# Attention on one core: a unit's row maxima computed beside the exponentials of the unit before it, without a lead of three score fills

## The chip, the cores and the metric

The kernel runs on one core of a Trainium2 chip. The metric is the device time of one execution in microseconds (us). Before the change three runs took 1225.27, 1232.97 and 1233.84 us, median 1232.97 us.

## The reference

Input `x` is 8 batches of 1024 tokens of width 256, float32. The reference is a block of three parts:

```
x = x + 0.5 * ffn(layernorm(x))      # 8 experts, top 2, each expert kept only if at most 1280 tokens chose it
x = x + attention(layernorm(x))      # 16 heads of width 16, causal
x = x + 0.5 * ffn(layernorm(x))
```

An expert that more tokens chose than its capacity is left out altogether. The kernel counts the choices while it computes the attention, and runs the expert part only if some expert is kept; in the profiled execution none is, so that all the time goes to the attention with its layer norms, gates and projections:

```
q, k, v = x @ Wq.T + bq, x @ Wk.T + bk, x @ Wv.T + bv
attn    = softmax(causal(q * 0.25 @ k.T))
out     = (attn @ v) @ Wo.T + bo
```

## The kernel before, in words

**Units.** The attention is cut into NU = 32 units: unit u is batch b = u // 4 and group g = u % 4 of four heads. Each unit has two kinds of score fills, 18 of each, and a fill is one step of the schedule:

- A maxima fill (`m_steps`, L831) multiplies queries by keys into a pair of PSUM banks, tile `sm`, and VectorE reduces it to row maxima, tile `mx` (L870). Fills 0 to 17 belong to two halves of the queries, hf = 0 and hf = 1; the last one of half 0 is fill 6, that of half 1 is fill 17.
- An exponential fill (`e_steps`, L928) computes the scores again, transposed, tile `sc`, and adds the negated maxima to them in TensorE (L947: `take_m` times the rows 62 to 66 of `neg`). ScalarE takes the exponential into `pT` (L966), GpSimd masks blocks on the diagonal, and `values` (L1000) multiplies `pT` by the values into `pav`. Fills E0 to E4 are half 0, E5 to E17 are half 1. E5 is the first that reads the maxima of half 1.

`sm` and `sc` share one PSUM pool of three pairs (L605): a fill can start when the reader of the fill three places earlier is done.

**From maxima to rows.** When a half's maxima are complete, `settle` (L888) runs four small VectorE operations (`mxr`, two on `mneg`, the transpose to `mside`) and starts `send` (L911). `send` issues two DMAs of 16 KB from ScalarE's queue: `rows` (SBUF to DRAM) and, when that has landed, `neg` (DRAM into the four rows of `neg`). `start(steps, lag)` (L1229) sets the step at which a sequence goes on: (3 * lag + 2) // 4 steps later. So `rows` is issued 2 steps after `mside`, and `neg` 5 steps after `rows`. Both stand in ScalarE's instruction order: while ScalarE's queue waits to issue `neg`, no later exponential is issued.

**Order of the work.** Everything is put into one hand-made order per engine (`Lane`, L615). Unit u's loop (L1311) runs "EMEMEM" six times: an exponential fill of unit u, then a maxima fill of the stream, 36 steps. The stream (`maxima`, L1245) goes through the maxima fills of all units in turn. Before unit 0 it runs the 18 fills of unit 0 alone; beside unit 0's exponentials it runs those of unit 1. At the start of unit 1 three more maxima fills are run alone (L1307 to L1309), so that from there on the stream is three fills ahead: beside unit u's exponentials stand fills 3 to 17 of unit u + 1 and fills 0 to 2 of unit u + 2. In unit 30 the stream ends three fills early, and unit 31 has exponentials only. Every third step `gap` (L1205) adds pieces of other work: the projections `pq` (L740), the values `pv`, the output projection `px`, the transposes `pta` of the normed input (`enter`, L716), and the products `pav` that have come due. `take(side)` adds small VectorE work, `settle` first.

**Loads.** SyncE's queue issues all large DMAs in order: `parts` (a projection's result to DRAM, four of 256 KB for each chunk, `project`), `qk` (back into SBUF, four of 512 KB for each unit: two tensors for each of two head pairs, `fetch`, L769), `sums`, `on`, `few`, `rs` (division by the row sums), `x_a` and `out_dram`. Unit u + 2's `qk` go to one of three buffers, whose last reader is unit u - 1; they are started 6 steps into unit u, and 5 steps apart.

Of the kernel before, what the change touches and what calls it, by code (L numbers as in the profile page):

```python
# [29 lines left out]
def macaron_kernel(  # L30
# [568 lines left out]
    def attention(run_no, src, dst, gate0, logits, tally):  # L599
        NU = B * NG  # L600
# [3 lines left out]
        with stack:  # L604
# [29 lines left out]
            def pair(name):  # L634
                return ps_pair.tile([P, 2, 512], F32, tag="pair", name=name)
# [10 lines left out]
            def matmul(out, lhsT, rhs, start=True, stop=True):  # L646
                on.tensor.matmul(out, lhsT=lhsT, rhs=rhs, start=start, stop=stop)
# [183 lines left out]
            def m_steps(u):  # L831
                q, k = qks[u % 3][:, 0], qks[u % 3][:, 1]

                def fill(hf, pieces):
                    sm = pair("sm{}_{}_{}_{}".format(u, *pieces[0][:3]))
                    ends = [at + (ib + 1) * P - j0 for ib, j0, pr, at in pieces if (ib + 1) * P - j0 <= 512]
                    for n, (ib, j0, pr, at) in enumerate(pieces):
                        w = min(512, (ib + 1) * P - j0)
                        for h in range(2):
                            r = 64 * h  # L840
                            matmul(
                                sm[:, h, at : at + w],
                                q[r : r + 64, pr, ib * P : (ib + 1) * P],
                                k[r : r + 64, pr, j0 : j0 + w],
                                start=(n == 0),
                                stop=not ends,
                            )
                    for c in range(2 if ends else 0):
                        for h in range(2):
                            r = 64 * h  # L850
                            at = ends[0] - P + 64 * c
                            part, mask = sm[:, h, at : at + 64], masked[r : r + 64, :]
                            if len(ends) == 2:
                                blocks = sm[:, h].rearrange("p (n w) -> p n w", w=P)[:, :, 64 * c : 64 * c + 64]
                                i0, i1 = (e // P - 1 for e in ends)
                                part = blocks[:, i0 : i1 + 1 : i1 - i0]
                                mask = mask.unsqueeze(1).to_broadcast([64, 2, 64])
                            matmul(part, before_k[r : r + 64, c, :], mask, start=False, stop=(c == 1))
                    mx = mx_tiles[u % 3][hf]
                    ib, j0, pr, at = pieces[0]  # L860
                    own = j0 == 512 * hf
                    if len(pieces) == 1:
                        g = (0, 2, 1, 3)[ib % 4]
                        out, in_ = mx[:, :, pr, g, (0 if own else (0, 1, 3, 1)[ib % 4])], sm
                    elif pieces[1][2] == pr:
                        flat = mx[:, :, pr].rearrange("p h g s -> p h (g s)")
                        out, in_ = flat[:, :, 3:7], sm.rearrange("p h (n w) -> p h n w", w=P)
                    else:
                        out, in_ = mx[:, :, :, 2, 0], sm.rearrange("p h (n w) -> p h n w", w=2 * P)
                    on.vector.tensor_reduce(out, in_, AX.X, ALU.max)  # L870

                plain = [(1, [(ib, 0, pr, 0)]) for ib in range(4, 8) for pr in range(2)]
                masked_ones = []
                for hf in range(2):
                    i, j0 = 4 * hf, 512 * hf
                    masked_ones.append([(hf, [(i + 3, j0, pr, 0)]) for pr in range(2)])
                    masked_ones[hf] += [(hf, [(i, j0, pr, 0), (i + 2, j0, pr, P)]) for pr in range(2)]
                    masked_ones[hf] += [(hf, [(i + 1, j0, 0, 0), (i + 1, j0, 1, 2 * P)])]
                if u == 0:
                    todo = masked_ones[0] + plain + masked_ones[1]  # L880
                else:
                    rest = deque(masked_ones[0] + masked_ones[1])
                    plain = deque(plain)
                    todo = [(plain if n % 3 == 1 or not rest else rest).popleft() for n in range(18)]
                steps = [lambda a=a: fill(*a) for a in todo]
                done = max(n for n, a in enumerate(todo) if a[0] == 0)

                def settle(hf):  # L888
                    mx = ap.tile([P, 4, 2, 2], F32, tag="mxr", name=f"mxr{u}_{hf}")
                    on.vector.tensor_reduce(  # L890
                        mx.rearrange("p x b a -> p x a b"),
                        mx_tiles[u % 3][hf].rearrange("p h r (a b) s -> p (h r) a b s", a=2),
                        AX.X,
                        ALU.max,
                    )
                    yield
                    mx = mx.rearrange("p (h r) b a -> p h (r b a)", h=2)
                    neg = ap.tile([P, 2, 2, 8], F32R, tag="mneg", name=f"mneg{u}_{hf}")
                    high, low = neg[:, :, 0], neg[:, :, 1]
                    on.vector.tensor_scalar(high, mx, -1.0, None, ALU.mult)  # L900
                    yield
                    on.vector.scalar_tensor_tensor(
                        low.bitcast(F32), mx, -1.0, high.bitcast(F32), ALU.mult, ALU.subtract
                    )
                    yield
                    turned = ap.tile([P, 32], F32, tag="mside", name=f"mside{u}_{hf}")
                    on.vector.transpose(turned, neg.bitcast(F32).rearrange("p x c i -> p (x c i)"))
                    start(send(hf, turned), 3)
                    yield

                def send(hf, turned):  # L911
                    rows = passing.tile([8, 512], F32, tag="rows", name=f"rows{u}_{hf}")
                    on.scalar.dma_start(out=rows.rearrange("c (i s q) -> s c i q", i=4, s=4), in_=turned)
                    yield 6
                    on.scalar.dma_start(
                        out=negs[u % 2][hf][62:66, :, :512].bitcast(F32),
                        in_=rows.rearrange("(p r) s -> p r s", r=2),
                    )

                return steps, settle, done  # L920


# [295 lines left out]
            def step(fill, every, rate, small):  # L1218
                due()
                fill()  # L1220
                count[0] += 1
                small, urgent[0] = max(small, urgent[0]), 0
                for _ in range(small):
                    if take(side):
                        break
                if count[0] % every == 0:
                    gap(rate)

            def start(steps, lag=0):  # L1229
                timed.append([count[0] + (3 * lag + 2) // 4, steps])  # L1230

            def due():
                for entry in list(timed):
                    while entry[0] <= count[0]:
                        lag = next(entry[1], None)
                        if lag is None:
                            timed.remove(entry)
                            break
                        entry[0] = count[0] + (3 * lag + 2) // 4
# [20 lines left out]
            for u in range(-1, NU):  # L1260
                b, g = divmod(u, NG)
                rate, every = 17 / 12, FILLS
                if u < 0:
                    rate, every = 23 / 9, 2
                elif g == 0:
                    spare[0] = False
                    if b == 0:
                        work.append(project(0, 1))
                        rate = 8 / 3
# [18 lines left out]
                elif g == 3:  # L1288
# [5 lines left out]
                    if b + 1 == B:  # L1294
# [3 lines left out]
                        rate = 8 / 3  # L1298
# [4 lines left out]
                if u < 0:  # L1303
                    for _ in range(18):
                        step(maxima, every, rate, 1)
                else:
                    if u == 1:  # L1307
                        for n in range(3):
                            step(maxima, every, rate, n)  # L1309
                    es = deque(e_steps(u))  # L1310
                    for k, which in enumerate("EMEMEM" * 6):  # L1311
                        small = 3 if k % 6 in (1, 5) else 0
                        if which == "E":
                            step(es.popleft(), 2 if u + 1 == NU else every, rate, 0 if u + 1 < NU else 2)
                        elif stream[0] < 18 * NU:
                            step(maxima, every, rate, small)
# [81 lines left out]
```

## Time and profile before

| | before |
|---|---|
| three runs, us | 1225.27, 1232.97, 1233.84 (median 1232.97) |
| the profiled execution, us | 1243.32 |
| span of its trace, us | 1241.2 |
| mean granted TensorE clock | 0.964 |
| busy, us (share of the span): TensorE | 1143.7 (92%) |
| VectorE | 939.9 (76%) |
| ScalarE | 739.6 (60%) |
| GpSimd | 434.8 (35%) |
| maxima reductions on VectorE (`mx`) | 576, mean 1216 ns |
| exponentials on ScalarE (`pT`) | 576, mean 1023 ns |

How to read it: PE is TensorE's matmuls, PEld its weight loads, DVE VectorE, ACT ScalarE, POOL GpSimd, SP SyncE; a q behind a name is the engine's queue, which issues DMAs. In a timeline, a row is a run of equal instructions: start and length in us, engine, line, operation, result <- operands, shapes, number, and in brackets how long the engine had been idle before it and what ended that. A wait put down to "issue" is one for which the profile shows no releaser. All operations that go through `Lane` carry line L623. PEclk is the clock that TensorE was granted, as a share of its full clock. Times are from the start of the span.

### The profile page before, as it was taken

What the parts mean: (1) busy time and instruction counts of PE and PEld (TensorE: products, weight loads), DVE (VectorE), ACT (ScalarE), POOL (GpSimd) and SP (SyncE); (2) the same over time, 40 slices, a digit from 0 to 9 for tenths busy, and PEclk for the clock granted to TensorE, in tenths of its full rate; (3) what the DMA queues carried; (4) which work ended last, traced back from release to release, by engine and by line L of the source; (5) the groups of instructions that cost most, each with busy time, mean ns of one, the idle gap of its engine ahead of it and who ended that gap; (6) DMA issues with size and microseconds to landing.
All of it is one profiled execution on the core that took longest, in us unless ns stands there. A gap on an engine that the chain in (4) does not pass through costs nothing.

```text
span 1241.2 us, 36200 instructions
## 1 busy us (share of the span) xinstructions
PE 1143.7 (92%) x15178; PEld 668.6 (54%) x15178; DVE 939.9 (76%) x1649; ACT 739.6 (60%) x955; POOL 434.8 (35%) x773
## 2 busy tenths in 40 slices
PE   4698999999999998999899998999989999999982
PEld 2455555555565554655456555655546555555541
DVE  2487668878698777888688787988778886798923
ACT  3155676666576565675566655765656655665650
POOL 2434233343344233442334433342344413232331
PEclk9698999999899998999999999999999999999997
DMA  3634674363555545353653635555553545543201
GB/s 108 234 123 167 208 224 130 119 231 105 189 153 158 187 153 189 119 182 134 214 168 112 221 112 194 148 161 189 164 192 113 185 137 182 156 126 105 83 19 38
DMA packets 108501, 190.25 MB, mean 153 GB/s; under 512 B 24736, under 2 KB 42280, under 8 KB 108328
## 3 DMA queue, kind: packets, MB, share of 16 engines
q1 hardware_dynamic: 96776, 184.54, 45.6%
q10 hardware_dynamic: 11552, 3.29, 1.2%
q8 instruction: 122, 2.00, 0.6%
q14 instruction: 51, 0.42, 0.1%
HBM read 94.50 MB, written 93.31 MB: 151 GB/s over the span
## 4 chain that ended last, share of the span: by engine, by line
PE 79%; DVE 10%; DMA 4%; issue 3%; ACT 2%; POOL 1%; ACTq 0%; SPq 0%; POOLq 0%; DVEq 0%
PE sc L623 23%; PE pav L623 21%; PE sm L623 16%; PE pq L623 8%; DVE mx L623 7%; PE px L623 4%; PE pv L623 4%; DMA rows<-mside 3%; PE pta L623 2%; ACT pT L623 1%; DMA parts<-low 1%; DVE mneg L623 0%; DVE st_a L623 0%; DVE xn_a L623 0%; DMA qk<-parts 0%
## 5 line engine op out<-in xcount | busy, mean ns | idle before, releaser
L623 DVE TENSOR_REDUCE mx<-sm 128x2 f32<-128x1024 f32 (+2 forms) x576 | 685.2, 1216 | 211.9 <-PE sm L623 186.0
L623 ACT ACTIVATE pT<-sc 128x1024 f32<-128x1024 f32 x576 | 575.0, 1023 | 329.7 <-PE sc L623 284.6
L623 POOL TENSOR_SCALAR_AFFINE_SELECT pT<-pT 128x256 f32<-128x256 f32 (+1 forms) x448 | 190.7, 440 | 496.0 <-ACT pT L623 485.4
L623 PE MATMUL pav<-pT,vaug 128*32 128x256 f32 (+3 forms) x4608 | 325.8, 390 | 1.4 <-ACT att L623 1.4
L623 PE MATMUL sm<-qk 64*128 64x512 f32 (+3 forms) x1536 | 266.9, 385 | 38.3 <-issue 20.7
L623 PE MATMUL sc<-neg,take_m 64*128 64x512 f32 x1152 | 266.8, 459 | 6.9 <-DVE mx L623 3.5
L623 PE MATMUL sc<-qk 64*128 64x512 f32 (+3 forms) x1536 | 230.9, 337 | 0.0
L623 PEld LDWEIGHTS sm<-qk 64*128 64x128 f32 x1536 | 142.1, 189 | 139.1 <-issue 69.8
L623 PEld LDWEIGHTS pav<-pT,vaug 128*32 128x32 f32 x4608 | 113.6, 109 | 103.4 <-issue 54.7
L623 PEld LDWEIGHTS sc<-neg,take_m 64*128 64x128 f32 x1152 | 110.5, 188 | 100.4 <-issue 50.3
L623 PEld LDWEIGHTS sc<-qk 64*128 64x128 f32 x1536 | 147.6, 188 | 16.5
L623 POOL TENSOR_TENSOR low<-whole,high 128x512 f32<-128x512 f32 x64 | 82.0, 1281 | 157.1 <-ACT high L623 146.2
L623 PE MATMUL sm<-masked,before_k 64*128 64x128 bf16 (+1 forms) x1280 | 87.2, 215 | 0.0
L623 PE MATMUL pq<-xnT,wkT 128*32 128x256 f32 x1024 | 75.7, 405 | 0.0
L623 PE MATMUL px<-woT,on 128*32 128x264 f32 x1024 | 73.7, 387 | 0.9 <-ACT on L623 0.9
L623 PE MATMUL pv<-wvT,xnT 128*32 128x264 f32 x1024 | 74.0, 391 | 0.0
L623 PE MATMUL pq<-xnT,wqT 128*32 128x256 f32 x1024 | 72.7, 389 | 0.5 <-ACT xnT L623 0.5
L623 PEld LDWEIGHTS <-before_k 64*128 64x128 bf16 x1280 | 38.3, 97 | 43.8 <-issue 27.5
L623 POOL TENSOR_TENSOR x_a<-x_a,bo_all 128x512 f32<-128x512 f32 x32 | 41.5, 1301 | 57.5 <-DVE xn_a L623 36.5
L623 PE MATMUL pta<-ident,xn_a 128*32 128x128 f32 (+1 forms) x912 | 33.9, 278 | 18.3 <-DVE xn_a L623 18.1
L623 PEld LDWEIGHTS pq<-xnT,wkT 128*32 128x32 f32 x1024 | 34.4, 115 | 28.0 <-issue 10.8
L623 PEld LDWEIGHTS pq<-xnT,wqT 128*32 128x32 f32 x1024 | 33.2, 112 | 27.8 <-issue 10.8
(128 smaller groups left out, 734.3 us busy)
## 6 DMA issues: line engine op xcount, KB each, us to landing
qk<-parts SPq DMA_DIRECT2D x124, 512.0 KB
parts<-high SPq DMA_DIRECT2D x128, 256.0 KB
parts<-low SPq DMA_DIRECT2D x128, 256.0 KB
sums<-att SPq DMA_DIRECT2D x62, 256.0 KB
x_a<-in_L_attn_x_dram SPq DMA_DIRECT2D x16, 512.0 KB
out_dram<-x_a SPq DMA_DIRECT2D x16, 512.0 KB
on<-sums SPq DMA_DIRECT2D x30, 256.0 KB
rs<-inv SPq DMA_DIRECT2D x30, 256.0 KB
```

The costliest lines, as they stand in the source:

```text
L623: i = call(*args, **kwargs)
```

## The change

Three edits:

1. The three maxima fills at the start of unit 1 are taken out. The stream is then exactly one unit ahead: beside unit u's exponentials stand fills 0 to 17 of unit u + 1. The fills themselves stay the same in number and form.
2. For the last unit, `rows` is started with lag 1, not 3: 1 step after `mside`, not 2.
3. For the last unit, `neg` follows `rows` with lag 4, not 6: 3 steps later, not 5.

```diff
                     on.vector.transpose(turned, neg.bitcast(F32).rearrange("p x c i -> p (x c i)"))
-                    start(send(hf, turned), 3)
+                    start(send(hf, turned), 3 if u + 1 < NU else 1)
                     yield
...
                     on.scalar.dma_start(out=rows.rearrange("c (i s q) -> s c i q", i=4, s=4), in_=turned)
-                    yield 6
+                    yield 6 if u + 1 < NU else 4
                     on.scalar.dma_start(
                         out=negs[u % 2][hf][62:66, :, :512].bitcast(F32),
...
                 else:
-                    if u == 1:
-                        for n in range(3):
-                            step(maxima, every, rate, n)
                     es = deque(e_steps(u))
```

In the order of instructions of the changed program, ScalarE's `rows` of half 1 stands behind E0 of the unit that needs it (before: behind E15 of the unit ahead), and `neg` behind E3 (before: behind E0). For half 0 `rows` stands behind E7 and `neg` behind E10 of the unit ahead (before: E4 and E7). Some pieces of the work that `gap` and `take(side)` place move by a few steps as well: in units with g = 1 the projection's last chunk stands behind E2 instead of E4, in units with g = 2 the first chunk behind E5 instead of E7, both halves of `out_dram` come ahead of `sums` on SyncE, and in units with g = 0 the normed inputs `xn_a` for the last `pta` stand on VectorE directly behind one `mx`, with no `settle` ahead of them.

## The prediction

> **What bounds the kernel now.** I read the page first (engine shares, the slices, the chain that ended last), then the waits of TensorE (PE), then the timelines around the longest of them.
>
> ```profile
> PE   4698999999999998999899998999989999999982
> PEclk9698999999899998999999999999999999999997
> ...
> PE 79%; DVE 10%; DMA 4%; issue 3%; ACT 2%; POOL 1%; ACTq 0%; SPq 0%; POOLq 0%; DVEq 0%
> ```
>
> From slice 4 to the last but one PE is busy nine tenths of the time, and it carries 79% of the chain. So the end moves only by what PE idles, and by what it loses when its clock falls. The waits of PE (releaser: us in total, times, longest):
>
> ```profile
> PE sm L623 <- issue: 20.7, 7, 4.1
> PE pta L623 <- DVE xn_a L623: 18.1, 9, 6.7
> ...
> PE sm L623 <- ACT pT L623: 4.5, 4, 2.1
> ...
> PE sc L623 <- DMA neg<-rows: 1.7, 1, 1.7
> ```
>
> The first line is one place in six units: the third maxima fill of the lead (fill 2 of unit u + 2, the first on the second head pair) stands at the end of the units with g = 2, ahead of its fourth `qk` load. PE's timeline there, and the windows behind all six (us; busy PE, PEld, DVE, ACT, POOL; PEclk; DMA share; GB/s):
>
> ```profile
> 762.17 0.50 PE L623 MATMUL sm<-qk 64*128 64x512 f32 x2 [3.47 <-issue]
> ```
> ```profile
> 326.30:332.60 6.30, 6.29 (x50) 3.37 (x54) 3.08 (x5) 1.53 (x2) 0.41 (x1) 0.50 0.48 179
> 472.80:479.40 6.60, 6.60 (x54) 3.56 (x58) 3.37 (x7) 1.86 (x2) 0.41 (x1) 0.51 0.39 146
> 618.00:622.70 4.70, 4.70 (x36) 2.66 (x38) 1.55 (x3) 0.77 (x1) 0.00 (x0) 0.50 0.52 199
> 762.10:766.10 4.00, 3.93 (x32) 2.15 (x34) 1.55 (x3) 0.30 (x1) 0.00 (x0) 0.57 0.53 202
> 906.10:909.50 3.40, 3.37 (x26) 1.68 (x28) 1.55 (x3) 0.00 (x0) 0.00 (x0) 0.51 0.55 206
> 1049.60:1056.20 6.60, 6.60 (x54) 3.55 (x58) 3.35 (x7) 1.88 (x2) 0.41 (x1) 0.50 0.34 129
> ```
>
> After each gap the granted clock stands near one half for 3.4 to 6.6 us: a gap costs its length and about 2.5 us more.
>
> **What the change gives (us of PE's time).**
> - A. The six gaps at the lead's third fill: 2.99, 4.07, 3.86, 3.47, 3.73, 2.17, together 20.3. After the change that fill comes six steps later, about 6 us at some 36 us for 36 steps, more than the longest gap: the load has landed. Gain 20.3.
> - B. The half clock behind them: length times the missing share, 3.15 + 3.23 + 2.35 + 1.72 + 1.67 + 3.30 = 15.4.
> - C. Six waits of `pta` for `xn_a`, 1.31 each (at 668.74, for one), are 7.9 of the 18.1. VectorE runs `settle` of half 0 ahead of that `xn_a` (0.22 + 0.18 + 0.62 + 0.21, about 1.25); in the changed order no settle stands there. Gain 7.9.
> - D. ScalarE waits at the issue of `neg` for `rows` to land, and the exponential behind it holds a PSUM pair (`sm <- ACT pT`, 4.5, with 1.7 of half clock after 138.0). I take 5; it may also stay, since `rows` keeps its lag: bounds 0 and 6.2.
> - E. The last unit's 1.73 wait for `neg`, 1.7 of half clock behind it. With the shorter lags its `rows` stands one step and its `neg` three steps sooner than the new place alone would give, which makes up for half of the six steps that the maxima come later, while units ahead of it make up for none. I take 1, bounds -3 (a stall of 3 in place of the 1.73, both with clock behind) and 3.4 (both gone).
>
> Sum of the gains 20.3 + 15.4 + 7.9 + 5 + 1 = 49.6. The three fills taken from the start of unit 1 run in unit 30, where PE has other work beside them just as there: 0.
>
> **What it takes.** E5 of every unit needs `neg` of half 1, which is now issued behind E3 of the same unit. Before, it was issued behind E0, with some 10 us to spare. What is left is read from unit 18: the scores of E3 end at 732.57, E5 begins at 735.63.
>
> ```profile
> 732.17 0.40 PE L623 MATMUL sc<-qk 64*128 64x384 f32 x4
> ...
> 735.63 0.40 PE L623 MATMUL sc<-neg,take_m 64*128 64x512 f32 x2
> ```
>
> That is 3.06; in other units 2.6 to 3.1 (2.2 to 2.4 in units 28 and 30). Behind E5 stand PE's maxima fills and products, so all of PE waits, and DVE and ScalarE after it. The transfer is quick when nothing is ahead of it, and slow otherwise. From the chain of waits (start, length):
>
> ```profile
> 397.27 7.13 DMA rows<-mside
> ...
> 976.09 7.00 DMA rows<-mside
> ...
> 1183.07 2.11 DMA neg<-rows
> ```
>
> Both transfers are 16 KB. What makes 7 of 2: SyncE's queue shortly before one `neg`, and that `neg` on ScalarE's queue:
>
> ```profile
> 267.18 1.22 SPq L623 DMA_DIRECT2D parts<-high  x2
> 268.54 1.97 SPq L623 DMA_DIRECT2D parts<-low  x2
> 270.57 1.50 SPq L623 DMA_DIRECT2D qk<-parts  x1
> ```
> ```profile
> 271.08 0.63 ACTq L623 DMA_DIRECT2D neg<-rows  x1
> ```
>
> In the DMA view of 271.1 to 275.6 only SyncE's queue shows packets:
>
> ```profile
> q1 hardware_dynamic: 475, 1.07, 80.7%
> ```
>
> ScalarE's queue (q10) shows its twelve packets from 275.6 to 276.6. So `neg` landed some 5.4 after its issue, when what SyncE had issued ahead of it was through. Four `parts` of 256 KB hold it about 1.4 each.
>
> - F. Units 7, 11, ..., 27 (g = 3; 6). Four `parts` are issued 4.5 to 6.4 after the unit's start (769.53 and 770.90 where it starts at 764.5); the new `neg` follows at about 7.0. The `parts` are through at about 11.3, it lands at 12.0 to 12.7, and E5 wants it at 9.4: stall 2.6 to 3.3, I take 2.9. Gaps of 2.12 (at 135.51) and 2.17 (at 1047.39) were followed by half clock, gaps of 0.9 to 1.3 were not; so 2.4 more. 5.3 x 6 = 32 (bounds 8, with 1.3 a unit, to 41).
> - G. Units 1 and 2, whose chunks stand behind E1, in the same way: 4.5 x 2 = 9 (4 to 14).
> - H. Units 6, 10, ..., 26 (g = 2; 6). Both halves of `out_dram` (512 KB each), `sums` and `qk` are issued ahead of `neg`: by the same rate a stall of about 2.2, and half clock after some of them, 0.8 on average: 3.0 x 6 = 18 (0 to 30).
> - I. The 17 other units: quiet transfer 2.11 against 2.2 to 3.1. I take 0.25 each, 4 (0, if always quiet, to 48 with a loaded one, see below).
>
> ScalarE's wait at `neg` delays what stands behind it, the exponential E4, only as long as `rows` is late; that is in D. POOL's masks follow the exponentials and wait for nothing new. The moved pieces of projections and `values` are the same instructions on the same engines; their cover is PE's own work, 0.
>
> Losses 32 + 9 + 18 + 4 = 63; net 63 - 49.6 = +13.5. The profiled execution would go from 1243.3 (span 1241.2 and 2.1 around it) to about 1257. It was 10 longer than the median of the runs; against 1232.97 the sum gives 1246.5, and I say 1247.
>
> [...] The gaps of 2.12 and 2.17 above lost half the clock. [...] The empty stretch of q10 from 271.1 to 275.6 shows a small transfer kept behind large ones. [...]
>
> **The rivals.**
> - Quick `neg` (ends faster). If `neg` lands within the 2.6 to 3.1 after E3 in nearly all units, F, G and H are gone and I is 4 to 10: 1233 - 49.6 + 7 = 1190. For it: the 2.11 at 1183.07. Against it: 7.13, 7.00 and the stretch from 271.1. It is decided by one number, the time from the issue of `neg` to its landing in units with g = 3: under 3 it is this case.
> - Cancelled out. `out_dram` is issued late enough, or its 512 KB packets let `neg` pass: H is 0, and 63 - 18 - 49.6 = -4.5, about 1229. For it: the order of SyncE's and ScalarE's queues in time is not fixed by the program. Against it: `sums` and `qk` are large as well.
> - Loaded everywhere. If `qk` loads of SyncE's queue, which fill the DMA for much of each unit (45.6% on the page), hold `neg` to about 4.5 in the other 17 units too, each has a stall of 1.6 to 1.9 and 1.0 of clock: 17 x 2.8 - 4 = 44 more, 1290. For it: 5.55 at 1096.48, in the last batch. Against it: `qk` of a unit are 5 steps apart, and in the mean engines are idle half the time.
> - That the change does not do what it says can be left out: the order of the instructions shows the fills moved.
>
> **How the numbers follow.** What a measurement of this kernel can tell from no change is about 1%, 12.3 us. The forecast has 0.42 (own range 1238 to 1262; of this 0.32 slower by over 1%, 0.10 within), cancelled out 0.22 (within 1%), quick `neg` 0.20 (faster), loaded everywhere 0.16 (slower). So faster 0.20, within 0.32, slower 0.48. The range from 1189 to 1285 leaves out about half of the quick and half of the loaded case, 0.18 in all.
>
> **What would show it.** A and B: no `sm` wait put down to "issue" in the g = 2 units, and no half clock at their ends. C: PE's waits for `xn_a` fall by six. F to H: a new line "PE sc <- DMA neg<-rows" among PE's waits, some 14 times 2 to 3 us, at E5, with half clock behind it. If that line is under 15 us in all, the losses are wrong; if the first line stays near 20, the gains are.

## The result, and the profile after

The changed kernel takes 1305.78 us, median of six runs (1297.09 to 1310.24), against 1233.4 (six runs, 1225.27 to 1237.16): ratio 1.0588, 95% interval 1.054 to 1.0637. It is slower, as forecast, but by 72 us and not by 13. The profiled execution took 1297.09 (span 1295.2), so the two traces differ by 54.0. The trace of before is one of its longer executions and that of after the shortest of six. The executions of both kernels spread, and the shorter ones have the higher granted clock: those of the kernel before, also in later runs, had spans from 1226.9 (clock 0.972) to 1242.1 (0.961), those of the changed one from 1295.2 (0.950) to 1308.4 (0.946). What follows accounts for the 54; the other 18 lie in executions that left no trace.

The page of after, busy slices of PE, its clock, and the chain that ended last:

```profile
PE   4798989989999899998999899998999899999983
PEclk9598989989999898999999899998989989999997
...
PE 68%; DMA 14%; DVE 13%; issue 2%; POOL 1%; ACT 1%; SPq 0%; ACTq 0%; POOLq 0%; DVEq 0%
```

PE's share of the chain fell from 79% to 68%, DMA's rose from 4% to 14%, and the dips of the clock come more often. PE's waits of after (releaser: us in total, times, longest):

```profile
PE sc L623 <- DMA neg<-rows: 61.8, 23, 5.5
...
PE pta L623 <- DVE xn_a L623: 10.5, 3, 6.7
...
PE sc L623 <- DVE mx L623: 9.1, 14, 2.3
...
PE sm L623 <- ACT pT L623: 0.7, 1, 0.7
```

The line `sm <- issue` (20.7 before) is gone, `pta` fell by 7.6 and `sm <- ACT pT` by 3.8: the gains came as forecast. In their place stands the wait for `neg`, 1.7 before and 61.8 now. By the page, PE's idle time rose by 32.9 (97.5 to 130.4) and its busy time by 21.1 (1143.7 to 1164.8), with the same number of instructions. Of these 21.1, 14.5 is clock: half of the time that PE was busy in half-clock pieces is 29.2 before and 43.7 after. The other 6.6 is not. Matmuls of `sc <- neg` at full clock add 191.7 after and 184.1 before, most of the difference at E5 (240 ns each in place of 133), where the first of them follows a wait.

Where the 61.8 lie is read from the timelines. In unit 5 (g = 1, starts at 263.33) SyncE's queue, ScalarE's queue and PE show:

```profile
263.07 0.57 SPq L623 DMA_DIRECT2D parts<-high  x1
264.44 0.57 SPq L623 DMA_DIRECT2D parts<-low  x1
265.36 0.57 SPq L623 DMA_DIRECT2D parts<-high  x1
265.98 1.11 SPq L623 DMA_DIRECT2D parts<-low  x1
...
271.57 1.21 SPq L623 DMA_DIRECT2D parts<-high  x2
272.94 1.95 SPq L623 DMA_DIRECT2D parts<-low  x2
```
```profile
266.55 0.54 ACTq L623 DMA_DIRECT2D rows<-mside  x1
...
273.59 0.65 ACTq L623 DMA_DIRECT2D neg<-rows  x1
```
```profile
278.64 0.79 PE L623 MATMUL sc<-neg,take_m 64*128 64x512 f32 x2 [5.04 <-DMA neg<-rows]
```

`rows` is issued behind four `parts` (the first rows) and lands 7.0 us later; only then can ScalarE issue `neg`, now behind four more `parts`, and E5 starts 5.05 after that. PE has waited 5.04. Two windows of this trace (us; busy PE, PEld, DVE, ACT, POOL; PEclk; DMA share; GB/s): while `neg` is under way the DMA engines are half busy, and behind the wait the clock is at one half:

```profile
273.00:277.00 4.00, 0.59 (x6) 0.19 (x2) 1.23 (x1) 1.02 (x1) 1.26 (x3) 0.87 0.50 148
```
```profile
278.70:282.80 4.10, 4.10 (x36) 2.35 (x36) 1.23 (x1) 1.02 (x1) 0.25 (x1) 0.50 0.69 262
```

The same for all units, from PE's timeline at E5 and the half-clock pieces there. These are 3.41 or 6.83 us long, and the long ones begin while PE still waits, so that only the time in which PE was busy counts (half of it is lost). The wait of unit 19 (2.33) ended with a reduction `mx`, not with `neg`. The last column is what the prediction had for these units, under the letters of its terms:

| units | waits at E5, us | sum | clock lost | together | forecast |
|---|---|---|---|---|---|
| g = 1: 5, 9, ..., 25 | 5.04 4.86 3.70 5.14 5.45 5.43 | 29.6 | 12.9 | 42.5 | 1.5 (in I) |
| g = 3: 7, 11, ..., 27 | 2.88 3.00 2.13 2.33 2.63 2.10 | 15.1 | 7.7 | 22.8 | 32 (F) |
| g = 2: 6, 10, ..., 26 | 2.23 2.30 1.25 0.96 0 0.95 | 7.7 | 3.4 | 11.1 | 18 (H) |
| 1 and 2 | 3.96 2.89 | 6.9 | 4.6 | 11.5 | 9 (G) |
| eleven others | up to 1.59 | 3.6 | 0 | 3.6 | 2.8 (in I) |
| 31, the last | 1.48 | 1.5 | 1.7 | 3.2 | in E |

### The profile page after: what moved, and what is told of

Same layout as the page of the kernel before. It is cut to its first block, busy times and chain, and to the rows that moved or that the text cites. A ratio compares the mean times of both kernels' runs of the same rounds, so it can differ in the third digit from the quotient of the medians.

```text
span 1295.2 us, 36221 instructions
## 1 busy us (share of the span) xinstructions
PE 1164.8 (90%) x15178; PEld 680.4 (53%) x15178; DVE 943.8 (73%) x1649; ACT 739.8 (57%) x955; POOL 434.0 (34%) x773
## 4 chain that ended last, share of the span: by engine, by line
PE 68%; DMA 14%; DVE 13%; issue 2%; POOL 1%; ACT 1%; SPq 0%; ACTq 0%; POOLq 0%; DVEq 0%
PE sc L623 20%; PE pav L623 19%; PE sm L623 13%; DVE mx L623 8%; DMA neg<-rows 8%; PE pq L623 7%; DMA rows<-mside 4%; PE pv L623 4%; PE px L623 3%; PE pta L623 2%; DVE mneg L623 1%; DMA parts<-low 1%; DVE x_a L623 1%; DMA qk<-parts 1%; DVE st_g L623 0%
## 5 line engine op out<-in xcount | busy, mean ns | idle before, releaser
L623 PE MATMUL sc<-neg,take_m 64*128 64x512 f32 x1152 | 272.2, 468 | 73.9 <-DMA neg<-rows 61.8
L623 PE MATMUL pav<-pT,vaug 128*32 128x256 f32 (+3 forms) x4608 | 333.7, 397 | 1.4 <-ACT att L623 1.4
L623 PE MATMUL sm<-qk 64*128 64x512 f32 (+3 forms) x1536 | 269.6, 388 | 13.6 <-DMA qk<-parts 12.6
L623 PE MATMUL sc<-qk 64*128 64x512 f32 (+3 forms) x1536 | 234.0, 340 | 0.0
L623 PEld LDWEIGHTS sm<-qk 64*128 64x128 f32 x1536 | 149.4, 193 | 115.1 <-issue 52.0
L623 PE MATMUL pq<-xnT,wkT 128*32 128x256 f32 x1024 | 70.0, 380 | 0.0
L623 PEld LDWEIGHTS <-before_k 64*128 64x128 bf16 x1280 | 39.6, 98 | 45.4 <-issue 29.2
L623 PEld LDWEIGHTS pv<-wvT,xnT 128*32 128x32 f32 x1024 | 32.7, 114 | 30.9 <-issue 11.9
L623 PEld LDWEIGHTS px<-woT,on 128*32 128x32 f32 x1024 | 33.0, 113 | 30.1 <-issue 10.8
```

The lines of the kernel that those rows point to most:

```text
L623: i = call(*args, **kwargs)
```

## The experiments

Theory 1 is that the loss is the short way of `neg` of half 1: `rows` and `neg`, issued behind E0 and E3, stand behind `parts` in the DMA engines. Theory 2 is that it comes from the pieces of other work that the missing lead moves. Ratios are to the kernel before on the same chip, with 95% intervals.

### The place of rows and neg alone, with the lead kept

```diff
-                    start(send(hf, turned), 3)
+                    start(send(hf, turned), 10 if hf and 0 < u < NU - 1 else 3)
```

> The kernel before, with its lead of three fills; only rows of half 1 is started with lag 10 instead of 3 (units 1 to 30), so that rows stands behind E0 and neg behind E3 of the unit that needs them, as in the changed kernel. All else stands where it stood. Theory 1 (the short way of neg is the loss): the waits of E5 for neg appear here too, in units with g = 3 and g = 2 as in the changed kernel, in units with g = 1 somewhat smaller because the last parts there come behind E4 instead of E2: 40 us and 25 us of half clock on top of the kernel before, 1298 us (1270 to 1330). Theory 2 (the loss is in the moved pieces or in the missing lead itself): no waits over 1 us at E5, 1228 to 1245 us.

1313.04 us, ratio 1.0608 (1.055 to 1.0666). PE's waits in this run:

```profile
PE sc L623 <- DMA neg<-rows: 55.3, 24, 9.8
PE sm L623 <- issue: 18.6, 6, 3.6
```

The wait for `neg` appears with the lead in place and every piece of other work where it was, and the gains (second line) do not. This is the loss of the changed kernel, most of it, without its gains; theory 2 falls as the main cause. One wait is this run's own: E5 of unit 1 waits 9.77, in the changed kernel 3.96. In units with g = 1 the waits are 2.15 to 4.29, smaller than the 3.70 to 5.45 of the changed kernel, where the last `parts` come two exponentials sooner and `rows` goes out 3.2 us after the unit's start, here 0.9. Which of the two makes the difference is not shown.

### Parts held back until E5 has its maxima

The `parts` that would be issued from 6 steps before a unit's start to 10 steps behind it go to step 10 or later. The memset of that step on GpSimd holds them back: a small DMA ahead of them on SyncE's queue waits for it.

```diff
...
+                if gated:
+                    on.gpsimd.memset(gate, 0.0)
+                    on.sync.dma_start(out=gate_d, in_=gate[0:1, :])
+                for c in range(4):
+                    part = (high, low)[c // 2 if t else c % 2]
...
```

> The changed kernel; the parts of a chunk that would be issued from 6 steps before a unit's start to 10 steps behind it are put off to step 10 or later, and a tiny DMA ahead of them waits for a GpSimd memset of that step, so that SyncE can't run ahead. Theory 1: rows and neg of half 1 have the DMA engines to themselves in units with g = 1 and g = 3: E5's waits there (30 and 15 us) go, and some 27 us of half clock: 1234 us (1212 to 1255). Rival (the parts are not what holds neg): E5's waits stay over 30 us in all, 1285 to 1312 us.

1272.24 us, ratio 1.0301 (1.0237 to 1.0365): half of the expected gain.

```profile
PE sc L623 <- DMA neg<-rows: 35.4, 21, 2.9
...
PE sm L623 <- ACT pT L623: 12.3, 8, 2.4
```

Where it was aimed it worked: E5 waits 0.0 to 0.1 in units with g = 3 (2.5 on average without the gate) and 0.7 to 1.3 in those with g = 1 (4.9). In the latter both transfers became shorter: from the issue of `rows` to that of `neg` 4.5 us (6.1 to 7.1 without the gate), from there to E5 3.2 to 3.8 (4.6 to 5.6). But the rest of SyncE's queue slid behind the gated `parts`: in units with g = 0 from 8 to 24, `rs`, `few` and `on`, which had gone out some 5 us ahead of the unit's start, now go out 2 to 4 us ahead of `neg`, where `sums` and a `qk` load stood already, and E5 waits 1.8 to 2.9 there, where it had waited 0 to 0.3.

### The same parts, eight steps later in the order only

The edit is that of the gate without the memset and its DMA, with `start(shipping, 10)` for every chunk of batch 1 and later.

> The changed kernel with the four parts of every chunk (from batch 1 on) issued 8 steps later on SyncE's queue; nothing moves on the other engines. Theory 1 (rows and neg stand behind parts): E5's waits in units with g = 1 (5.0 us each) and g = 3 (2.5 us each) are gone, 45 us, and with them about 27 us of half clock; those in units 1 and 2 and with g = 2 stay. 1306 - 72 = 1234 us (1215 to 1250). Theory 2 (moved pieces on PE, DVE and ScalarE): the pieces stand where they stood, 1290 to 1312 us.

1305.72 us, ratio 1.0549 (1.0456 to 1.0642), and 60.7 us of waits for `neg`: in sum nothing changed. SyncE's queue has no clock. It went on to the next DMA when its data was there, and in units with g = 1 that was as early as before: the first `parts` for unit 5 were issued at 261.65, ahead of that unit's start at 261.90, and E5 still waits 4.7 to 5.2. In units with g = 3 the `parts` did move, from 4.9 us after the unit's start to 9.1 or later, which is behind `neg`. There E5 waits 0.1 in units 11, 19 and 27, but 5.3 and 5.1 in units 15 and 23, where ScalarE issued `neg` 1.2 to 1.9 us later and so behind two `qk` loads. Units 11 and 15 (SyncE's loads, `neg`, E5):

```profile
505.20 0.63 ACTq L623 DMA_DIRECT2D neg<-rows  x1
506.08 1.08 SPq L623 DMA_DIRECT2D qk<-parts  x2
507.67 0.50 PE L623 MATMUL sc<-neg,take_m 64*128 64x512 f32 x2
...
657.37 0.87 SPq L623 DMA_DIRECT2D qk<-parts  x2
658.01 0.63 ACTq L623 DMA_DIRECT2D neg<-rows  x1
664.19 0.79 PE L623 MATMUL sc<-neg,take_m 64*128 64x512 f32 x2 [5.33 <-DMA neg<-rows]
```

The total says nothing for or against either theory; unit by unit it fits theory 1, with large loads of any kind ahead of `neg`.

### Four more large DMAs ahead of neg, in three ways

In each unit with g = 0, four DMAs of 256 KB (weights to unused DRAM) are released by a GpSimd memset behind the mask of E1 (or of E4).

```diff
+            def load_dma():
+                on.gpsimd.memset(extra, 0.0)
+                on.sync.dma_start(out=extra_d[4, 0:1, 0:8], in_=extra[0:1, :])
+                for c in range(4):
+                    on.sync.dma_start(out=extra_d[c], in_=wqT.rearrange("p c d -> p (c d)"))
...
+                            if g == 0 and 0 < u and k == 2:
+                                load_dma()
```

> The changed kernel with four more DMAs of 256 KB (weights to unused DRAM) on SyncE's queue in each unit with g = 0 from unit 4 on, released behind the mask of E1, so that they are issued shortly ahead of neg. E5 of these seven units waits for nothing so far. Theory 1: what is issued ahead holds neg, so E5 there waits 2 to 4 us each, with half clock behind some: 20 to 40 us more than the changed kernel, 1326 to 1346 us. Rival (a small transfer takes turns with large ones, and neg is late for another reason): the waits there stay under 1 us, 1300 to 1315 us.

> The same four more DMAs, released behind the mask of E4, so that they are issued after neg. Theory 1: neg is ahead of them and lands as before: E5 in units with g = 0 waits under 1 us, and the time is that of the changed kernel, 1300 to 1316 us. Rival (it is the load on the DMA engines at the time, not what was issued ahead): E5 waits 1 to 3 us there too, 1315 to 1340 us.

1312.04 us ahead (ratio 1.059, 1.0525 to 1.0654) and 1309.01 behind (1.0591, 1.0523 to 1.0659). Ahead of `neg` they cost hardly anything: only unit 4 waited (3.58), the others at most 0.24. A window of this run over the four transfers shows why: all 16 DMA engines are busy (share 0.99), and at 369 GB/s the 1.05 MB are through in 2.8 us, before `neg` needs them.

```profile
396.50:399.00 2.50, 2.50 (x43) 1.69 (x36) 2.29 (x4) 2.08 (x4) 1.40 (x2) 1.00 0.99 369
```

`parts` go at the share 0.50 and 148 GB/s shown above, so that four of them take some 7 us. So the third run wrote the same bytes in the shape of `parts` (`extra_d[c, :, 0]` of a tile `[5, 8, 2, 16, 512]`).

> [...] Theory 1, made exact (neg uses engines that parts uses, and these work in the order of issue): the four take 5.6 us, neg is held 2 to 4 us and E5 of the seven units waits 2 to 4 us each, with half clock behind some: 1322 to 1348 us. Rival: E5 there waits under 1 us, 1300 to 1315 us.

1346.94 us, ratio 1.0903 (1.0852 to 1.0954). While the four were under way (391.0 to 396.0, ahead of unit 8's E5) the DMA share was 0.50 at 149 GB/s, which makes 7.0 us for them in place of the 5.6 expected. That `neg` uses engines that `parts` uses, and that these work in the order of issue, was the author's assumption; no trace shows it. E5 of unit 8 in this run:

```profile
399.12 0.50 PE L623 MATMUL sc<-neg,take_m 64*128 64x512 f32 x2 [4.42 <-DMA neg<-rows]
```

All seven units with g = 0 wait now, 2.04 to 4.63, together 26.3. Two delays add up there. In six of the seven `neg` was issued 1.4 to 2.1 us late (unit 8: 8.99 after the start of the unit, 7.00 in the changed kernel): in the trace its issue waits on the DMA semaphore that the first of the four counts on, and goes at 393.60, when that one ends (393.58). From its issue to E5 it then takes 4.4 to 5.7 (3.0 to 3.6 in the changed kernel). In the changed kernel the late issue in units with g = 1 is not this one: there `neg` waits for `rows` to land.

### Shorter lags in all units, and without the shorter lags

```diff
-                    start(send(hf, turned), 3 if u + 1 < NU else 1)
+                    start(send(hf, turned), 1)
...
-                    yield 6 if u + 1 < NU else 4
+                    yield 4
```

> The changed kernel with the short lags (1 and 4) in every unit: rows stay behind E0, neg goes from behind E3 to behind E1. Theory 1: ScalarE waits at neg until rows has landed, but neg is then issued about +4.5 us into the unit instead of +7, ahead of most parts in units with g = 3 and of the loads in g = 2: the waits there go (2.5 and 1.3 us each, six units each, and their half clock). In units with g = 1 rows itself stands behind parts, so that neg goes no sooner, and E5 waits about 5 us as before. 1306 - 46 + 10 for blocked exponentials = 1270 us (1250 to 1290). Theory 2 (moved pieces): no change, 1298 to 1314 us.

1304.87 us, ratio 1.0599 (1.0573 to 1.0625): no gain. The wait for `neg` fell to 5.3 and another took its place:

```profile
PE sm L623 <- ACT pT L623: 54.7, 22, 5.5
```

ScalarE reaches `neg` before `rows` has landed, waits there (105.8 us in all), and the exponentials behind it keep PSUM pairs from PE. I had expected 1270 because I took the wait of ScalarE for the cheaper one. But the edit shortens the lags of both halves. Of the 54.7, 23.7 stand behind `neg` of half 1 (3.5 to 4.5 in each unit with g = 1 from 5 to 25, where `rows` is slow), and 31.0 behind `neg` of half 0, which had time to spare in the changed kernel (0.7 there). One of each kind, both in unit 21:

```profile
887.00 0.90 PE L623 MATMUL sm<-qk 64*128 64x128 f32 x4 [4.54 <-ACT pT L623]
...
906.29 0.51 PE L623 MATMUL sm<-qk 64*128 64x512 f32 x2 [3.32 <-ACT pT L623]
```

In units with g = 1 the way itself is too short, wherever ScalarE stands in the meantime. Whether shorter lags for half 1 alone would have paid was not tried; without the 31.0 it would be about 1274, an estimate from this trace.

The other way round, the three fills taken out and the lags of the last unit left at 3 and 6:

> The three maxima fills at the start of unit 1 taken out, the lags of the last unit as before (3 and 6). Theory 1: all the loss comes with the fills; the shorter lags save the last unit some 2 us of waiting: 1308 us (1298 to 1316), and only E5 of unit 31 waits longer, by 2 to 4 us. Rival (the shorter lags make ScalarE wait in the last unit and cost something): under 1295 us.

1307.28 us, ratio 1.0631 (1.0575 to 1.0686), with 65.0 us of waits for `neg`: edits 2 and 3 can't be told from nothing.

### A lead of one or two fills

```diff
-                        for n in range(3):
+                        for n in range(2):
```

> The kernel before, with two maxima fills at the start of unit 1 in place of three. Theory 1 (the way of neg is too short): neg of half 1 is issued behind E1 instead of E3, some 4 us sooner than without a lead, so that it lands in time even behind four parts: the waits of E5 for neg are under 5 us in all. The third fill of a unit, the first that needs the second head pair, is no longer run a unit ahead, so the six waits at the fourth qk load and the half clock behind them are gone as well: 1233 - 36 = 1197 us (1188 to 1210). Theory 2 (it is the pieces of projections that moved, not the place of neg): the pieces move nearly as they do without a lead, so most of the loss stays, 1270 to 1300 us.

> The kernel before, with one maxima fill at the start of unit 1 in place of three. Theory 1: neg of half 1 is issued behind E2, 2 us sooner than without a lead. Of the waits of E5 those in units with g = 2 and g = 3 go (2.5 and 1.3 us each), those in units with g = 1 go from 5 to about 3 us, with half clock behind: losses of about 40 us against gains of about 50, 1223 us (1205 to 1245). Theory 2 (moved pieces): 1270 to 1300 us.

1279.46 us with two (ratio 1.0391, 1.0366 to 1.0416) and 1333.56 with one (1.0829, 1.0802 to 1.0856). Both expectations failed. With two fills, PE's waits are:

```profile
PE sc L623 <- DVE mx L623: 45.0, 77, 1.7
...
PE sc L623 <- DMA neg<-rows: 2.6, 1, 2.6
```

The part of theory 1 that concerns `neg` holds (E5 waits for it in the last unit only), and so does that on the fourth `qk` load. But the exponential fills now wait for maxima reductions in many small gaps, 45.0 us (53.0 with one fill), against 3.5 before. The run that puts pieces and small VectorE work back behind the same kinds of fills:

> A lead of two fills, with the step counter put on by one after it and the small VectorE work tied to the kind of the maxima fill, so that pieces and small work stand behind the same kinds of fills as before. Theory 3 (in the run with a lead of two, the 45 us of waits of sc for mx come from pieces and small work that fell on other fills): these waits fall under 10 us, the waits for neg and qk stay away, 1197 us (1188 to 1215). Rival (they come from the exponential and maxima fills that now share the three PSUM pairs in another pairing): the waits stay over 30 us, 1260 to 1285 us.

1288.19 us, ratio 1.0415 (1.035 to 1.048), and 49.9 us of these waits: theory 3 falls. What is left is the pairing of exponential and maxima fills in the three PSUM pairs, which a lead of three or none keeps; that is only argued, no run shows it.

### The gain without the loss: the lead kept, the loads sooner

```diff
-                    start(fetch(u + 2, lag=6), 8)
+                    start(fetch(u + 2, lag=5), 4)
```

> The kernel before, with the lead of three, and the qk loads of the unit after next started 3 steps into the unit instead of 6, 4 steps apart instead of 5. If the six waits of the third lead fill are only the late fourth load, they and the half clock behind them go and nothing else changes: 1233 - 36 = 1197 us (1188 to 1212). Rival (SyncE's queue is held by what stands ahead of the loads, so that the fourth lands no sooner): over 1222 us.

1225.38 us, ratio 0.9918 (0.9892 to 0.9945): faster than both kernels, than the one before by 0.8%, less than expected. The waits at the fourth load and the half clock behind them are gone (the clock is 0.975), and PE's first waits are:

```profile
PE pta L623 <- DVE xn_a L623: 18.4, 9, 6.8
PE sm L623 <- ACT pT L623: 15.3, 16, 3.1
```

The second line was 4.5 before. Fifteen of its sixteen gaps end 1.8 to 1.9 us after a `neg` that ScalarE issued 5.7 to 9.2 us after its `rows`: ScalarE came to `neg` before `rows` had landed and held up the exponential behind it, as with the short lags. Which transfers hold `rows` there was not tried. With `neg` later (`yield 8` and `yield 9` for `yield 6`):

> The kernel before with the earlier qk loads, and neg started with lag 8 after rows instead of 6 (6 steps, not 5). In the run with the earlier loads PE waited 15.3 us for exponentials that stood behind ScalarE's wait at neg for rows. If that wait is what it gave back, one step (1 us) takes away about half of it and E5, which has over 2 us left, waits for nothing new: 1225 - 8 = 1217 us (1210 to 1223). Rival (the time of rows and neg adds up, and E5 waits instead): 1225 to 1240 us.

> As before, with lag 9 (7 steps): about 2 us later than with lag 6. ScalarE's waits at neg are nearly gone, 1225 - 13 = 1212 us, if E5 still has time; with 5 us from issue to E5 in units with g = 1 and g = 3 and transfers of up to 5.6 us, waits of up to 1 us may begin there: 1208 to 1222 us. Rival: E5's waits for neg are 10 us or more in all, 1225 to 1245 us.

1225.64 (ratio 0.9925, 0.9898 to 0.9953) and 1217.91 (0.9863, 0.9836 to 0.989). One step more moved nothing (18.8 us of `sm <- ACT pT`; from the issue of `neg` to E5 of unit 11 there are 7.03 us, as with lag 6): steps alternate between the two kinds of fills, and only exponentials stand on ScalarE. Two steps put `neg` behind the next exponential, and PE's wait `sm <- ACT pT` fell from 15.3 to 0.2. What is left of `neg`:

```profile
PE sc L623 <- DMA neg<-rows: 11.1, 3, 5.9
```

These three waits are in units 0, 1 and 31; keeping lag 6 there was not tried.

## Why the prediction was wrong, point by point

- **What bounds the kernel, and the gains A to E: right.** A 20.7 (20.3 forecast), C 7.6 (7.9), D 3.8 and 1.7 of clock (5). B is 15.4 (15.4), counted as in the table above. The last unit gave some 1.6 (1): its E5 still waits 1.48 with half clock behind, but its first wait for a copy of `neg` on GpSimd (1.35) is gone. Together about 51 (49.6).
- **F, G and H: right in kind, off in size.** 22.8 for 32, 11.5 for 9, 11.1 for 18. The stalls of F were 2.5 on average (2.9 taken), and only three of six had half clock behind them, where I had put 2.4 on each. The late `parts` were shown to be the cause of F by the gate (g = 3: 2.5 to 0.1), and the waits of units 1 and 2 fell with it too (6.9 to 2.4). For H I had both halves of `out_dram` ahead of `neg`; in the trace the first goes out 9.8 us before the unit's start, and only the second, 4.6 after it, with `sums` and `qk`, stands near. No run moved these transfers, so that their part in H is only argued.
- **I: this step failed.** "The 17 other units: quiet transfer 2.11 against 2.2 to 3.1. I take 0.25 each". Six of the seventeen, those with g = 1, are not quiet: 42.5 in place of 1.5. The order of the changed program showed their last chunk behind E2 instead of E4, and I priced the chunk's move at nothing on its own engines without asking which transfers it puts ahead of the new places of `rows` and `neg`. I also priced only `neg`. In these units `rows` itself takes some 7.0 behind the first four `parts`, ScalarE's issue of `neg` waits for it, and `neg` then takes some 5.0 behind the next four: two waits in a row, both shorter with the gate. The moved chunk is not all of it: with the lead kept it stays behind E4 and `rows` goes out 2.3 us sooner, and these units still wait 3.2 on average.
- **The sum.** Losses 91.5 (63 forecast), gains 51: some 41. Two small terms that I did not have, the other waits of `sc` for `mx` (9.1, of which 2.3 is at E5 of unit 19, against 3.5: 3.3) and a longer half-clock piece at the start (30.72 us against 23.89: 2.6), bring it to 47 of the 54 between the traces. The other 7 are about the 6.6 by which PE was busy longer at full clock.
- **The rivals.** "Quick `neg`" is out by its own test: in units with g = 3 from 7 to 27 there are 4.8 to 5.6 us from the issue of `neg` to E5, where under 3 was asked. "Cancelled out" is out as well. "Loaded everywhere" came nearest in time (1290), but by the wrong units: it spread 2.8 over 17, and it was 7 in six of them and next to nothing in the others. My range ended at 1285 because I gave that case 0.16 and cut half of it.
- **The two readings that the losses rest on.** That gaps of 2.12 and 2.17 lose half the clock: over the sixteen traces of this study (without the first 110 us and the last 45), half clock began during the gap or within 3.41 us of its end (the shorter of the two lengths of half-clock pieces above) for 5 of 451 gaps of 0.4 to 1.5 us, 12 of 29 from 1.5 to 1.9, 46 of 56 from 1.9 to 2.5, 48 of 58 from 2.5 to 3.41, and all 68 longer ones. The reading held for most gaps of that length; the change lies between 1.5 and 2 us here. That `neg` is kept behind `parts`: in the changed kernel E5 of the units with g = 1 begins 4.6 to 5.6 us after the issue of `neg`, with the `parts` held back 3.2 to 3.8.

## What to carry to other kernels

When a change moves a small transfer later, read for every kind of unit what the other queues issue in the few microseconds ahead of its new place, and price the whole chain of transfers that leads to it, not the last one alone. A place in an order is no time: SyncE's queue ran ahead when its data was there (`parts` put eight steps later still went out 0.25 us ahead of unit 5), and what is moved may land on a neighbour that was quiet (behind the gate E5 of units with g = 0 waited 1.8 to 2.9 us, before that 0 to 0.3). A lead that looks like a cost (here 36 us of waits at a late load and half clock behind them) may be what hides a transfer; look first whether the late load itself can come sooner, which here gave 0.8% with the lead kept, and 1.4% together with a later `neg`.

## What the runs showed of the hardware

- Equal bytes did not take equal times. Four transfers of 256 KB written as 128 rows in a row kept the DMA share at 0.99 and moved 369 GB/s (2.8 us for the four); in the shape 8 x 16 rows it was 0.50 and 148 GB/s, some 7 us for the four. The prediction had taken 1.4 for each of these, and at 148 GB/s it is 1.8. The traces do not show which engine a packet took.
- A DMA's issue waited for an older one on another queue: `neg` stood on ScalarE's queue until the end of a transfer of SyncE's that counts on the same semaphore (393.58, with the issue at 393.60, in the run with parts-shaped transfers; also in unit 1 of the changed kernel, 9.15 and 9.17 after its start).
